# A gated cross attention kernel: scores moved behind the last attention segment, bias added in DRAM, inner sums moved ahead of three additions

## The chip, the cores and the metric

The kernel runs on one core of a Trainium2 chip. A core has five engines that run their own instruction streams side by side: TensorE (PE, matrix products; its weight loads are shown apart, as PEld), VectorE (DVE), ScalarE (ACT), GpSimd (POOL) and SyncE (SP, which here issues DMAs). The metric is the device time of one execution in microseconds, lower is better.

## What is computed

With `x` of 8 x 1024 x 1024 and a memory `ctx` of 8 x 64 x 512, all in float32:

```python
memory_proj = einsum('bme,de->bmd', memory, W_mem)
scores = einsum('bnd,bmd->bnm', x, memory_proj) / sqrt(D)
attn = softmax(scores, axis=-1)
memory_context = einsum('bnm,bmd->bnd', attn, memory_proj)
gate_input = concatenate([x, memory_context], axis=-1)
gate = sigmoid(einsum('bnf,df->bnd', gate_input, W_gate) + b_gate)
fused = x + gate * memory_context
out = fused * rsqrt(mean(square(fused), axis=-1) + 1e-6) * norm_w
```

D is 1024, M (the rows of memory of a batch) is 64. The large product is `x` by the first half of `W_gate`, 8192 x 1024 x 1024. The second half of `W_gate` is folded into the memory first: `mg = memory_proj @ W2` for each batch, so that `attn @ mg` gives what the concatenated half contributes, with the bias added to the rows of `mg` (the rows of `attn` sum to 1).

## The kernel before

**Quads and products.** The rows of `x` go through in 16 *quads* of 512 rows, two to a batch (`QPB` is 2, `NQ` is 16). The large product of a quad is done by a scheme of Strassen's kind, on two levels. On the outer level, seven products replace eight. They run in the order 1, 6, 7, 5, 4, 2, 3 (`ORDER`), and each is computed by `outer_product` (line 746). On the inner level, each outer product is again seven products of 128 x 256 blocks, named A, B, C, D, A (added onto the first), E and F; each of these takes one *slot* of TensorE. A quad has 49 slots.

**The left sides.** The four parts of the transposed `x` of a quad are `a11`, `a12`, `a21`, `a22` (`A[q, r, h]`), made by VectorE's transposes (`transpose_x`, line 335) out of the loaded rows `xq`. The sums that the outer products need, `S1` to `S4`, are VectorE's work over 1024 elements (`outer_s`, line 350): S1 = a21 + a22, S2 = S1 - a11, S3 = a11 - a21 (written in place of a21), S4 = a12 - S2. Outer product 7 takes S3 and outer product 3 takes S4. The sums for the inner products, four to an outer product in a tile `l2`, are GpSimd's work (`inner_s`, line 379), in two parts of two sums; B needs the first part, C and F the second.

**What follows a product.** ScalarE copies the first A to `u` (line 803), VectorE adds B, C and D onto it (`u2`, `u3`, `u4`). `pre` (line 785) adds `u3` and `u4` onto the output tiles on GpSimd, three additions for most outer products and six for product 5. `fin` (line 791) adds the PSUM results onto them on VectorE. Five PSUM banks are passed round from product to product, so that a late `fin` holds up a later product. The output tiles (`gate`) come from a pool of 7.

**The attention.** `scores(q)` (line 391) multiplies the memory with the `a` tiles: 16 pairs of matmuls, each pair using two column halves of the array (the weights have 64 columns), and ScalarE copies the result `psT`. It is emitted at slot 7 of the quad, between outer products 1 and 6. `transpose_scores`, `softmax_a`, `softmax_b`, `transpose_attn` and `attn_difference` follow at slots 9 to 21. In the last four outer products (5, 4, 2, 3), between the second A and E, stands a segment `pc` (line 820): eight pairs of matmuls, each on two row halves of the array (contraction over 64), which multiply the attention with the memory (`pc`) and with `mg` (onto A, F, E and D). Then ScalarE applies the sigmoid, and VectorE multiplies with `pc` (`gated`).

**The order of the work.** Nothing is left to a scheduler: `pin` keeps program order on every engine. `plan` (line 598) writes work into two lists. `at(slot, fn)` puts it into a slot, counted from `t0 = 49 * q`; it is emitted just before that slot's product. `mid((q, o), fn)` puts it into the middle of outer product `o` of quad `q`, behind the `pc` segment and before E. Later, `outer_product` itself plans `gated`, the residual (line 652, a GpSimd DMA that adds `x` onto the output tile while it loads), `square` (ScalarE) and `norm` (VectorE), which stores the tile. An engine runs its stream in order, so an instruction that waits holds up everything behind it on the same engine.

**The memory's side.** `mgd` is a DRAM tile of 2 x 512 x 1024: `mgd[0]` holds `memory_proj` and `mgd[1]` holds `mg` for all batches. `load_mg` (line 462) brings the 64 rows of each for a batch into one SBUF tile `mgs[b]`, at the beginning of the batch. `add_bias` (line 467) then adds the bias onto the upper 64 partitions by an accumulating GpSimd DMA, at slot 8 of the first quad of each batch, 8 times in all.

Of the kernel before, what the change touches and what calls it, by code (L numbers as in the profile page):

```python
# [10 lines left out]
ALU = mybir.AluOpType  # L11
# [4 lines left out]
P = 128  # L16
# [4 lines left out]
def tile_gated_cross_attention_rmsnorm(  # L21
# [42 lines left out]
    nc = tc.nc  # L64
    B, N, D = x.shape
    M, E = mem.shape[1:]
    QT = 4 * P
    QPB = N // QT
# [20 lines left out]
    pin = tc.keep_in_program_order  # L89
# [10 lines left out]
    def t4k(pool, shape, tag, name):  # L100
        return pool.tile(shape, F32, tag=tag, name=name)
# [33 lines left out]
    for k in range(KD):  # L135
        t = t4k(*((gpool, [P, D], "gate") if k < 7 else (apool, [P, D], "s4")), f"w2_{k}")
# [47 lines left out]
    mgd = dram.tile([2, BM, D], F32, name="mgd")  # L184
# [146 lines left out]
    sTs, attns, attnTs, scs, mps, mgs = {}, {}, {}, {}, {}, {}  # L331
# [132 lines left out]
        for g in range(2):  # L464
            load(mgs[b][g * M : (g + 1) * M, :], mgd[g, b * M : (b + 1) * M, :])

    def add_bias(b):
        pin(nc.gpsimd.dma_start(mgs[b][M:P, :], b_gate.partition_broadcast(M), accum_op=ALU.add))

# [116 lines left out]
    def at(slot, fn, *args):  # L588
        due.setdefault(slot, []).append(lambda: fn(*args))

    def mid(key, fn, *args):
        beside.setdefault(key, []).append(lambda: fn(*args))
# [5 lines left out]
    def plan(q):  # L598
        t0 = SLOTS * q
        nxt = q + 1 < NQ  # L600
        order = [o for o, _ in ORDER]
        for i, o in enumerate(order):
            for part, t in ((0, 1), (1, 5)):
                if i + 1 < len(order):
                    at(t0 + 7 * i + t, inner_s, q, order[i + 1], part)
                elif nxt:
                    at(t0 + 7 * i + t, inner_s, q + 1, order[0], part)
        at(t0 + 7, scores, q)
        at(t0 + 7, outer_s, q, 3)
        at(t0 + 7, outer_s, q, 4)  # L610
        at(t0 + 9, transpose_scores, q)
        at(t0 + 10, softmax_a, q)
        at(t0 + 13, softmax_b, q)
        at(t0 + 18, transpose_attn, q)
        at(t0 + 21, attn_difference, q)
        if not nxt:
            at(t0 + 5, load_last)
            return
        at(t0 + 2, load_xq, q + 1)
        for t in (2, 3):  # L620
            mid((q, 5), transpose_x, q + 1, t, 0)
            mid((q, 2), transpose_x, q + 1, t, 1)
        for i, t, half in ((36, 0, 0), (38, 1, 0), (43, 0, 1), (45, 1, 1)):
            at(t0 + i, transpose_x, q + 1, t, half)
        mid((q, 3), outer_s, q + 1, 1)
        mid((q, 3), outer_s, q + 1, 2)
        if (q + 1) % QPB == 0:
            at(t0 + 10, load_mp, (q + 1) // QPB)
            at(t0 + 49, load_mg, (q + 1) // QPB)
        if q % QPB == 0:  # L630
            at(t0 + 8, add_bias, q // QPB)

    for o in (2, 3):
        w1_place(o)
# [106 lines left out]
    def sqrt_table():  # L741

        t = t4k(small, [P, 1], "warm", "warm")
        pin(nc.scalar.activation(t, eps_sb, AF.Sqrt))  # L744

    def outer_product(q, o, ext):
# [113 lines left out]
        if o in (4, 3) and q + 1 == NQ:  # L860
            c, d = 2 * ext[0], 2 * ext[0] + 1
            if o == 3:
                sqrt_table()
            when = (4, 5, 7, 9, 11, 12) if o == 4 else (2, 4, 5, 6, 7, 8)
            at(slot + when[0], last_root, d)
            at(slot + when[1], last_root, c)
            for w_, (t, h_) in zip(when[2:], ((d, 0), (d, 1), (c, 0), (c, 1))):
                at(slot + w_, last_norm, t, h_)
        elif o in (4, 3):

            row = ext[0]
            c, d = 2 * row, 2 * row + 1
            for t in (d, c):
                at(slot + 5, residual, q, t)
            if row == 0:
                when = (17, 18, 23, 29, None, None)
            else:
                when = (17, 18, 23, 25, 26, 28)
            at(slot + when[0], square, q, c)
            at(slot + when[1], square, q, d)  # L880
            for w_, (t, h_) in zip(when[2:], ((c, 0), (c, 1), (d, 0), (d, 1))):
                if w_ is None:
                    mid((q + 1, 4), norm, q, t, h_)
                else:
                    at(slot + w_, norm, q, t, h_)
# [3 lines left out]
    for q in range(NQ):  # L889
        plan(q)  # L890
        for o, ext in ORDER:
            outer_product(q, o, ext)
# [29 lines left out]
```

## Time and profile before

| | |
|---|---|
| median of 3 runs | 974.6 us (974.18 to 974.84) |
| the profiled execution | 974.45 us, its span 972.7 us |
| TensorE busy | 961.5 us, 99% of the span |
| VectorE, GpSimd, ScalarE busy | 825.1, 763.4, 327.0 us |
| granted TensorE clock | 0.996 |
| scores (`psT`) | 512 matmul records, 16 x 32 |
| bias DMAs | 8, 256 KB each, 7.3 us to landing, 0.83 us of GpSimd each |
| residual DMAs | 60, 512 KB each, 8.2 us to landing (median) |
| from one quad's scores to the next | 55.05 us for most (87.12 to 142.31 is 55.19, 857.91 to 913.22 is 55.31) |

The *span* runs from the first to the last instruction of one execution that the hardware profiler recorded. A float32 matmul shows as two records, so a slot of two matmuls shows as four. In the chain of waits the profile follows what ended last back to the beginning; work that isn't in it was hidden. In a list of waits, a row says which engine and tile waited, for whom, how long in all, how often and how long at most. In a timeline a row has start, duration, engine, line, operation, tiles, shape and count; the ends of matmuls are modelled, so their starts are what counts. Rows with "issue" show idle time in which nothing recorded was waited for.

### The profile page before, as it was taken

The numbers are of one execution on the slowest core, as the hardware profiler recorded it, in microseconds if no ns is written. First come the engines' busy times: TensorE is split into PE (matmuls) and PEld (weight loads), VectorE is DVE, ScalarE is ACT, GpSimd is POOL, SyncE is SP. The second block draws the span as 40 slices with busy tenths as digits, with TensorE's granted clock in tenths as the row PEclk, the third lists the DMA queues.
The fourth block names the chain that finished last, engine by engine and source line by source line (L and its number), as shares of the span: only waits on it lengthen the run. The fifth ranks groups of instructions, "written<-read, shape, count | busy, mean of one in ns | idle before, by whom it ended". The sixth has DMA issues, their size and how long they took to land.

```text
span 972.7 us, 14393 instructions
## 1 busy us (share of the span) xinstructions
PE 961.5 (99%) x4986; PEld 772.9 (79%) x4986; DVE 825.1 (85%) x1483; ACT 327.0 (34%) x603; POOL 763.4 (78%) x895
## 2 busy tenths in 40 slices
PE   9999999999999999999999999999999999999995
PEld 8546878888888888888887888888887888888884
DVE  5988888979797988979797988979797988979787
ACT  2000224251423334151433334161333334152355
POOL 4998878878687878878787877878787887878792
PEclk9999999999999999999999999999999999999998
DMA  9857183573819373482818374481918465391612
GB/s 377 267 145 167 18 139 92 121 170 79 177 59 177 116 130 98 111 183 68 181 65 163 109 142 109 99 194 57 192 65 152 121 130 119 87 206 47 181 77 86
DMA packets 71255, 128.32 MB, mean 132 GB/s; under 512 B 12432, under 2 KB 49296, under 8 KB 70928
## 3 DMA queue, kind: packets, MB, share of 16 engines
q1 hardware_dynamic: 61760, 93.34, 35.4%
q0 software_dynamic: 9280, 33.56, 18.7%
q8 instruction: 39, 0.64, 0.3%
q10 hardware_dynamic: 144, 0.52, 0.2%
q14 instruction: 32, 0.26, 0.1%
HBM read 87.56 MB, written 39.85 MB: 131 GB/s over the span
## 4 chain that ended last, share of the span: by engine, by line
PE 99%; DVE 0%; ACT 0%; DVEq 0%; issue 0%
PE kA L92 20%; PE pc L92 12%; PE kE L92 11%; PE kD L92 10%; PE kF L92 10%; PE kC L92 10%; PE kB L92 10%; PE psT L92 6%; PE pg L92 5%; PE pm L92 3%; PE pz L92 0%; PE sc L412 0%; PE pa L438 0%; PE pt L194 0%; DVE gate L737 0%; ACT L744 0%
## 5 line engine op out<-in xcount | busy, mean ns | idle before, releaser
L95 POOL TENSOR_TENSOR gate<-gate,u 128x256 f32<-128x256 f32 x336 | 271.9, 841 | 112.0 <-DVE u L95 106.4
L650 ACT ACTIVATE gate<-gate 128x512 f32<-128x512 f32 x128 | 78.9, 629 | 399.3 <-DVE gate L95 399.2
L95 POOL TENSOR_TENSOR l<-a 128x256 f32<-128x256 f32 x128 | 132.1, 1032 | 55.6 <-DVE a L95 55.6
L344 DVE STREAM_TRANSPOSE a<-xq 128x512 f32<-128x512 f32 x128 | 137.7, 1097 | 3.1 <-DMA mgd<-mpq 3.1
L92 PE MATMUL pc<-mg,attnT 64*128 64x256 f32 x512 | 127.4, 389 | 0.0
L679 DVE SCALAR_TENSOR_TENSOR gate<-gate,ss,nw_sb 128x512 f32<-128x512 f32 x120 | 125.6, 1056 | 1.1
L92 PE MATMUL kB<-it,l 128*128 128x256 f32 x448 | 115.1, 379 | 0.0
L92 PE MATMUL kD<-it,l 128*128 128x256 f32 x448 | 115.0, 379 | 0.0
L92 PEld LDWEIGHTS pc<-mg,attnT 64*128 64x128 f32 x512 | 90.6, 186 | 29.8 <-issue 21.2
L92 PE MATMUL kA<-w,a 128*128 128x256 f32 x384 | 98.6, 379 | 0.0
L92 PEld LDWEIGHTS kB<-it,l 128*128 128x128 f32 x448 | 85.0, 190 | 11.8 <-DVE gate L95 0.3
L92 PEld LDWEIGHTS kD<-it,l 128*128 128x128 f32 x448 | 85.1, 190 | 11.6
L95 DVE TENSOR_TENSOR gate<-gate,pc 128x512 f32<-128x512 f32 x128 | 87.0, 679 | 5.9 <-ACT gate L650 5.8
L92 PEld LDWEIGHTS kA<-w,a 128*128 128x128 f32 x384 | 71.7, 190 | 9.5 <-DVE mg_c L95 0.2
L95 POOL TENSOR_TENSOR l<-s 128x256 f32<-128x256 f32 x96 | 75.3, 785 | 4.0 <-PE kF L92 3.8
L803 ACT COPY u<-kA 128x256 f32<-128x256 f32 x112 | 40.5, 362 | 103.5 <-PE kA L92 102.4
L92 PE MATMUL kE<-it,a 128*128 128x256 f32 x256 | 69.0, 392 | 0.0
L92 PE MATMUL kA<-t,s 128*128 128x256 f32 x256 | 67.4, 386 | 0.0
L95 DVE TENSOR_TENSOR u<-u,kB 128x256 f32<-128x256 f32 x112 | 45.4, 405 | 25.8 <-PE kB L92 23.8
L92 PE MATMUL kC<-w,l 128*128 128x256 f32 x256 | 65.7, 379 | 0.0
L92 PE MATMUL kF<-w,l 128*128 128x256 f32 x256 | 65.7, 379 | 0.0
L664 ACT ACTIVATE junk<-gate 128x1024 f32<-128x1024 f32 x60 | 63.6, 1059 | 1.5 <-DMA gate<-in_x 0.5
(140 smaller groups left out, 2036.0 us busy)
## 6 DMA issues: line engine op xcount, KB each, us to landing
xq<-in_x SPq DMA_DIRECT2D x64, 512.0 KB, 9.7
gate<-in_x POOLq DMA_DIRECT2D x60, 512.0 KB, 8.2
out<-gate SPq DMA_DIRECT2D x60, 512.0 KB, 2.6
w<-in_w_gate_t SPq DMA_DIRECT2D x8, 512.0 KB, 10.9
w<-in_w_gate_t SPq DMA_DIRECT2D x2, 2048.0 KB, 16.9
mg<-mgd SPq DMA_DIRECT2D x16, 256.0 KB, 3.8
mpd<-mpT SPq DMA_DIRECT2D x4, 512.0 KB, 7.0
mgd<-mpq SPq DMA_DIRECT2D x16, 128.0 KB, 4.2
```

Source lines behind the costliest of these rows:

```text
L92: pin(nc.tensor.matmul(o, lhsT, rhs, start=start, stop=stop, skip_group_check=True))
L95: pin(eng.tensor_tensor(o, a, b, op))
L344: nc.vector.transpose(A[key][:, :, r * P : (r + 1) * P], chunks(xq[q][:, 4 * t : 4 * t + 4, :], KD)[:, half * KH : (half + 1) * KH],)
L650: pin(nc.scalar.activation(g, g, AF.Sigmoid))
L664: nc.scalar.activation(junk, O[q, t], AF.Square, accum_out=ss[:, t % 2 : t % 2 + 1])
L679: nc.vector.scalar_tensor_tensor(g[:, cols], g[:, cols], rstd[:, t % 2 : t % 2 + 1], nw_sb[:, cols], ALU.mult, ALU.mult,)
L803: pin(nc.scalar.copy(p1, kb["A"]))
```

## The change

It has five parts.

1. `scores(q + 1)` is emitted in the middle of outer product 3 of quad `q`, behind its `pc` segment, for all quads but the first, whose scores stay at slot 7.
2. The third and fourth outer sums, which were at slot 7 with the scores, go to slots 6 and 20 for all quads but the first.
3. Of the four transposes for the next quad with fixed slots, the last two go from slots 43 and 45 to 42 and 43.
4. The bias is added in SBUF for the first batch only. For the others one accumulating GpSimd DMA over 448 rows adds it in DRAM, onto `mgd[1, 64:]`, at slot 20 of the first quad.
5. The second part of the inner sums of the outer product behind 7 (which is 5) goes from slot 19 to slot 16, and with that ahead of the three additions of product 7. The last two norms of the tiles of outer product 4 go three and four slots back (`when`, 26 to 29 and 28 to 32).

```diff
-    def add_bias(b):
-        pin(nc.gpsimd.dma_start(mgs[b][M:P, :], b_gate.partition_broadcast(M), accum_op=ALU.add))
+    def add_bias(rows):
+        pin(
+            nc.gpsimd.dma_start(
+                rows, b_gate.partition_broadcast(rows.shape[0]), accum_op=ALU.add
+            )
+        )
...
-            for part, t in ((0, 1), (1, 5)):
+            for part, t in ((0, 1), (1, 2 if o == 7 else 5)):
...
-        at(t0 + 7, scores, q)
-        at(t0 + 7, outer_s, q, 3)
-        at(t0 + 7, outer_s, q, 4)
+        if q == 0:
+            at(t0 + 7, scores, q)
+        at(t0 + (6 if q else 7), outer_s, q, 3)
+        at(t0 + (20 if q else 7), outer_s, q, 4)
...
-        for i, t, half in ((36, 0, 0), (38, 1, 0), (43, 0, 1), (45, 1, 1)):
+        for i, t, half in ((36, 0, 0), (38, 1, 0), (42, 0, 1), (43, 1, 1)):
             at(t0 + i, transpose_x, q + 1, t, half)
+        mid((q, 3), scores, q + 1)
         mid((q, 3), outer_s, q + 1, 1)
         mid((q, 3), outer_s, q + 1, 2)
...
-        if q % QPB == 0:
-            at(t0 + 8, add_bias, q // QPB)
+        if q == 0:
+            at(t0 + 8, add_bias, mgs[0][M:P, :])
+            at(t0 + 20, add_bias, mgd[1, M:, :])
...
-                when = (17, 18, 23, 25, 26, 28)
+                when = (17, 18, 23, 25, 29, 32)
```

## The prediction

> **What bounds the kernel now.** I read the page first: busy times, then the chain that ended last.
>
> ```profile
> span 972.7 us, 14393 instructions
> ...
> PE 961.5 (99%) x4986; PEld 772.9 (79%) x4986; DVE 825.1 (85%) x1483; ACT 327.0 (34%) x603; POOL 763.4 (78%) x895
> ...
> PE 99%; DVE 0%; ACT 0%; DVEq 0%; issue 0%
> ```
>
> TensorE carries 99% of the chain. Only something that shortens TensorE's own sequence, or makes it wait, can count. Next, the waits, keeping TensorE's and those the change touches:
>
> ```profile
> PEld kE L92 <- issue: 21.2, 64, 0.3
> DVE a L95 <- PE psT L92: 23.1, 16, 1.5
> PEld kA L92 <- DVE a L95: 5.8, 15, 0.4
> PEld psT L92 <- issue: 5.3, 16, 0.3
> PEld kC L92 <- POOL l L95: 0.4, 1, 0.4
> ```
>
> Of TensorE's own, the `psT`, `kA` and `kE` rows recur in every quad at the same 0.3 to 0.4 us. They stand where the matmul's shape changes, so they are no data waits: the one called "DVE a" looks like the `kE` ones that wait for nothing. VectorE's 23.1 us behind `psT` is real, but VectorE is not in the chain. To price a shape change, the timeline of TensorE around a 64-row segment (`pc`) and around the 64-column scores (`psT`):
>
> ```profile
> 343.40 1.03 PE L92 MATMUL kA<-w,a 128*128 128x256 f32 x4
> 344.36 0.48 PE L92 MATMUL pc<-mg,attnT 64*128 64x256 f32 x1
> ...
> 344.68 0.38 PE L92 MATMUL pc<-mg,attnT 64*128 64x256 f32 x1
> ...
> 345.97 0.38 PE L92 MATMUL pc<-mg,attnT 64*128 64x256 f32 x1
> ...
> 346.29 1.13 PE L92 MATMUL kE<-it,a 128*128 128x256 f32 x4
> 347.25 1.03 PE L92 MATMUL kF<-w,l 128*128 128x256 f32 x4
> ```
>
> ```profile
> 361.47 1.03 PE L92 MATMUL kF<-w,l 128*128 128x256 f32 x4
> 362.42 3.67 PE L92 MATMUL psT<-a,mpb 128*64 128x256 f32 x32
> 366.03 1.13 PE L92 MATMUL kA<-t,s 128*128 128x256 f32 x4
> 366.99 1.03 PE L92 MATMUL kB<-it,l 128*128 128x256 f32 x4
> ```
>
> Starts are what to read. An undisturbed product of four records takes 0.863 us (347.25 to 348.12), 0.216 a record; two half-array records run side by side in 0.216.
> - `pc` segment: 343.40 to 347.25 is 3.85; two products (1.726) and 8 pairs (1.728) leave **0.40** for going in and out.
> - `psT` segment: 361.47 to 366.99 is 5.52; two products and 16 pairs (3.456) leave **0.34**.
> - Ways out: 345.97 to 346.29 is 0.32, so 0.10 over a pair; the next product starts after 0.96, another 0.10: 0.20. The way out of `psT` has the same 0.96 behind it. So the way into `pc` costs 0.40 - 0.20 = 0.20 and into `psT` 0.34 - 0.20 = 0.14. Both start 0.09 late; the rest is the first weights, unhidden (137 ns for 64 columns, 187 for 128, in the groups by shape).
>
> **What the skill says.** "TensorEngine Tiling (Array Packing)", Key Properties: "Mode switching requires drain", and it means a change of tiling mode. The trace agrees (0.14 to 0.20 a switch), but neither shows a switch from 64-row to 64-column tiles. "TensorE: Matmul & The Clock Gate", LDWEIGHTS pull-ahead in Step-by-step: weights load ahead while row groups don't conflict; between equal shapes the trace has weight loads 26 ns apart, at a switch 0.33 us. "GPSIMD Engine Reference", Specifications, lists its SBUF interfaces as shared with VectorE instructions that have two SBUF inputs; here the same GpSimd sum takes 0.72 to 1.05 us by what VectorE does. "DMA: Bandwidth & Descriptors", Queues, rings and completion order: each engine alternates between queues by packet; I use it for the accumulating loads below (their landing times rise from 5 to 15 us beside other loads, which fits).
>
> **The change, part by part.**
>
> *Scores moved (15 of 16 quads).* The same 32 records now follow the `pc` segment of the quad before, ahead of `kE`. Before, each quad paid 0.40 + 0.34. Now it pays the way into `pc` 0.20, one switch from row to column tiles, and the way out 0.20. That switch is not in the trace. Below: 0, if both tilings coexist; above: 0.34, as much as going out and in again; worse is conceivable only if it drains more than two switches do. I take 0.14, the way into `psT` (the drain of 0.09 and the same small weights). Saved: 0.74 - 0.54 = 0.20 a quad, 15 x 0.197 (unrounded) = **2.95 us**; ends 0 and 15 x 0.34 = 5.1. Scores need the second half of the transposes. VectorE runs them in slots 42 and 43 now: from `kF`'s sum at 348.39 in the same quad, transpose, `gated`, transpose end near 351.5, and the scores can start at 354.4: cover 2.9 us. ScalarE's copy of `psT` moves along, ahead of two sigmoids that wait for `kE` and `kF` anyway, 3.6 us later than before.
>
> *What that shifts.* Product 1 of the next quad runs 3.4 us later; from product 6 on all is 0.2 early again. So the cover that the scores gave at slot 7 is gone there and stands before product 1. GpSimd's residual DMA for tile 0 starts behind a VectorE product 2.6 us later (359.95 becomes 362.6). It landed 11 to 15 us after issue (7 in the last quad) and its square started 13.8 to 14.7 after; half of the quads have 0.0 to 1.1 us left. Its rival traffic (`xq`) starts about 1.1 us earlier, behind earlier transposes, and the bias DMA is gone from these quads, so the queues drain at about the same time. A square up to 1.1 us late is absorbed by ScalarE's 0.58 us wait before `u` and VectorE's own lag; TensorE needs the attention 2.3 us later.
>
> *Third and fourth outer sums, norms.* `outer_s 3` (1.22 us) no longer waits for `psT`; it ends at 366.65 instead of 365.65, for a GpSimd sum whose `kC` has 1.0 us of margin and gets its additions earlier too. `outer_s 4` (1.22) moves from behind `psT`'s wait, where it was free, to slot 20. The norm of slot 12 goes to slot 15, that of 14 to 18. All within VectorE's stretch from `u` of product 6 (368.13) to `u` of product 5 (380.66), which held 1.0 us of idle. After: it starts 0.4 earlier and holds 1.25 more work, so it ends near 380.8, 0.4 us later against TensorE. Behind it stand `u3` of product 5, GpSimd's six additions and the inner sum for `kC` of product 4. In before that sum ended 0.92 us ahead of its `kC` (387.62 against 388.55), bound by GpSimd's queue; 0.2 to 0.4 of it goes, 0.5 to 0.7 stays. Cost on the path 0.
>
> *Inner sums of product 5 ahead of three additions.* This is the tightest place before:
>
> ```profile
> 379.40 0.73 POOL L95 TENSOR_TENSOR l<-s 128x256 f32<-128x256 f32 x1
> ...
> 380.39 1.03 PE L92 MATMUL kC<-t,l 128*128 128x256 f32 x4
> ```
>
> 0.26 us of margin, -0.25 once (the `kC <- POOL` wait, at 875.96). The two sums (0.73 + 0.91) move into 1.54 us in which GpSimd waited for `u`, so they end some 3 us earlier and the additions hardly later. Gain: that one stall, **0.25 us**.
>
> *Bias.* Eight GpSimd DMAs of 64 rows (0.83 us each) become one of 64 and one of 448 rows into DRAM. Issue cost of 448: from 0.83 (64 rows) and 0.87 (128), an estimate of 1.1; 5.8 if it goes by row (0.83 x 448/64). In the first quad it stands before product 4's sums, where GpSimd idled 1.89 us (105.43 to 107.32), so 1.1 is free; 5.8 would cost TensorE 3.6 once, past the 0.3 us that product 4's `kC` has there. Transfer: 256 KB landed in 7.3 us, 512 in 8.2, so 1.8 MB in about 13 by that slope: landed before the first residual 17 us later, long before the next `mg` load 78 slots on. The gone DMAs save 6 x 0.83 us of GpSimd off the path.
>
> **The sum.** Profiled execution 974.45 us, span 972.7 (1.75 around it); 972.7 - 2.95 - 0.25 = 969.5 of span, 971.25 with what lies around. The median shown is 0.15 above the profiled execution: **971.4 us**, 0.33% less.
>
> **Rivals.** *The switch eats it:* going from row to column tiles costs 0.34 and only the stall of 0.25 is saved: 974.3, the same within 0.2% (about what a measurement of this kernel can tell from no change). For it: no such switch is in the trace. Against it: all four kinds seen cost 0.14 to 0.20. It turns from faster to same when the switch costs over 0.22. *Column tiles come free:* switch 0, 974.6 - 5.35 = 969.3. Against it: every change of shape has drained.
> *VectorE becomes late (slower):* place, `u3` of product 5 after `outer_s 4` and the moved norm; both lengthen beside GpSimd, the norm from 0.75 to 1.25. If the additional 1.25 us finds none of the 1.0 us idle and a norm takes 1.25 instead of 0.9, VectorE is 1.25 + 0.35 - 0.4 = 1.2 late, GpSimd's additions start so much later, and `kC` of product 4, with 0.7 us left, waits 0.5 in each of 15 quads: 7.5 on top, 978.9. It decides from a lateness of 0.7 (a stall) and 0.9 (15 x 0.2, the gain is gone). For it: VectorE is 85% busy and nearly without gaps there. Against it: the norms stay within the same stretch and its start is earlier.
> *The late residual:* squares wait over 3 us, the attention reaches `pc` late; 1 us in each of the 7 quads with `mg` loads, 978.4. Against it: the earlier `xq` and the missing bias DMA. *The change does nothing it says* is out: the instruction order has `psT` behind the last `pc` in 15 quads.
>
> **How the numbers follow.** Forecast 0.62 (switch 0.08 to 0.22, 970 to 972.6); free switch 0.07; switch eats it 0.17; VectorE late 0.08; residual or the long DMA 0.06, of which 0.02 still faster. Faster 0.62 + 0.07 + 0.02 = 0.71; same 0.17; slower 0.08 + 0.04 = 0.12. The range takes in the free switch's upper part and the equal case, and leaves out the slower ones: 969.5 to 974.6; the forecast's own is 970 to 972.6.
>
> **What would show it.** Quad period 54.85 instead of 55.05 us; the two `pc` and `psT` segments of a quad's end joined, the first `psT` 0.09 us late plus a first pair of 0.27; `PEld kA <- DVE a` from 5.8 to under 0.5; `DVE a <- PE psT` from 23.1 to about 1.5; no `kC <- POOL` in later quads; GpSimd's idle before product 7's additions gone. I am wrong if TensorE shows data waits of over 0.2 us in each quad, at `kC` of product 4 above all, or if the joint of the two tilings costs other than 0.14.

## The result and the profile after

The changed kernel takes **972.5 us** (median of 15 runs, 971.84 to 973.15), and the kernel before, run beside it, 974.5 us (15 runs, 973.95 to 974.97). The ratio is 0.998, with a 95% interval of 0.9973 to 0.9987: faster by 0.2%, or 2.0 us. The forecast was 971.4 us, so the gain is 1.2 us smaller than forecast. The profiled execution of the changed kernel took 972.48 us, its span is 970.7 us.

The page of the kernel after, its first lines and the chain that ended last:

```profile
span 970.7 us, 14400 instructions
...
PE 958.1 (99%) x4986; PEld 773.3 (80%) x4986; DVE 815.0 (84%) x1483; ACT 329.2 (34%) x603; POOL 763.5 (79%) x889
...
PE 97%; DVE 1%; DMA 1%; issue 0%; ACT 0%; DVEq 0%
```

TensorE still carries the chain. Its busy time fell by 3.4 us (961.5 to 958.1), the span by only 2.0: the rest stands as idle time. VectorE and a DMA at the kernel's start are in the chain now, with 1% each.

The list of waits of the kernel after (engine, tile, waited for what: us in all, times, longest us), keeping those of TensorE that changed and VectorE's wait for the scores:

```profile
PEld kE L92 <- issue: 22.0, 64, 0.4
PEld psT L92 <- issue: 5.3, 16, 0.3
DVE a L95 <- PE psT L92: 0.9, 1, 0.9
PEld kB L92 <- DVE gate L95: 0.8, 1, 0.8
PEld kC L92 <- POOL l L95: 0.5, 2, 0.3
PEld kA L92 <- DVE a L95: 0.4, 1, 0.4
PEld kD L92 <- DVE u L95: 0.4, 1, 0.4
```

The fifteen ways out of the scores, which stood as `kA <- DVE a` with 5.8 us before, are down to one. `psT` is as before and `kE` nearly so (21.2 before), so what went is one change of array mode in each of 15 quads. Of data waits inside the quads TensorE had two before, one at `kB` (0.3) and one at `kC` (0.4). Now there are four: `kB` once, `kC` twice, `kD` once. These are the losses.

The start times of TensorE's `sc` (the transposed scores) give a clock for the quads. The time from one quad's `sc` to the next:

| stretch | before | after | difference |
|---|---|---|---|
| up to the first `sc` | 92.48 | 92.45 | -0.03 |
| first quad | 55.19 | 55.54 | +0.35 |
| 13 quads between | 13 x 55.05 | 11 x 54.85, 54.91, 55.03 | -2.36 |
| last but one | 55.30 | 54.85 | -0.45 |
| from the last `sc` to TensorE's last matmul | 43.73 | 44.22 | +0.49 |
| sum | | | -2.00 |

The new joint, in TensorE's timeline of the kernel after (start, duration, engine, line, operation, tiles, shapes, count):

```profile
353.65 0.38 PE L92 MATMUL pc<-mg,attnT 64*128 64x256 f32 x1
353.66 0.38 PE L92 MATMUL kD<-mg,attnT 64*128 64x256 f32 x1
353.87 0.38 PE L92 MATMUL pc<-mg,attnT 64*128 64x256 f32 x1
353.88 0.38 PE L92 MATMUL kD<-mg,attnT 64*128 64x256 f32 x1
354.18 3.67 PE L92 MATMUL psT<-a,mpb 128*64 128x256 f32 x32
357.79 1.13 PE L92 MATMUL kE<-it,s 128*128 128x256 f32 x4
358.75 1.03 PE L92 MATMUL kF<-w,l 128*128 128x256 f32 x4
```

A pair of row halves takes 0.216 (353.65 to 353.87). From the last pair to the first `psT` it is 0.31 (353.87 to 354.18), so 0.09 late. From 354.18 to 357.79 the 16 pairs and the way out's first part take 3.61: 3.456 for the pairs, 0.05 for a first pair that is longer, and 0.10 to `kE`. The switch costs 0.09 + 0.05 = **0.14 us**, the value taken in the forecast; the second half of the way out (`kE` to `kF` 0.96 instead of 0.863) is there as before.

### The profile page after: what moved, and what is told of

Read it like the earlier page. It is cut to its first block, busy times and chain, and to the rows that moved or that the text cites. A ratio compares the mean times of both kernels' runs of the same rounds, so it can differ in the third digit from the quotient of the medians.

```text
span 970.7 us, 14400 instructions
## 1 busy us (share of the span) xinstructions
PE 958.1 (99%) x4986; PEld 773.3 (80%) x4986; DVE 815.0 (84%) x1483; ACT 329.2 (34%) x603; POOL 763.5 (79%) x889
## 4 chain that ended last, share of the span: by engine, by line
PE 97%; DVE 1%; DMA 1%; issue 0%; ACT 0%; DVEq 0%
PE kA L92 20%; PE pc L92 12%; PE kE L92 11%; PE kD L92 10%; PE kF L92 10%; PE kC L92 10%; PE kB L92 10%; PE psT L92 6%; PE pg L92 5%; PE pm L92 3%; DMA memq<-in_mem 1%; PE pa L438 0%; PE sc L412 0%; DVE gate L744 0%; DVE it L95 0%
## 5 line engine op out<-in xcount | busy, mean ns | idle before, releaser
L95 POOL TENSOR_TENSOR gate<-gate,u 128x256 f32<-128x256 f32 x336 | 287.5, 886 | 107.2 <-DVE u L95 107.2
L95 POOL TENSOR_TENSOR l<-a 128x256 f32<-128x256 f32 x128 | 124.6, 974 | 21.6 <-PE kA L92 20.4
L92 PEld LDWEIGHTS pc<-mg,attnT 64*128 64x128 f32 x512 | 90.6, 186 | 29.9 <-issue 21.2
L686 DVE SCALAR_TENSOR_TENSOR gate<-gate,ss,nw_sb 128x512 f32<-128x512 f32 x120 | 109.0, 918 | 1.1
L95 POOL TENSOR_TENSOR l<-s 128x256 f32<-128x256 f32 x96 | 79.3, 826 | 33.1 <-PE kF L92 30.3
L95 DVE TENSOR_TENSOR gate<-gate,kE 128x256 f32<-128x256 f32 x112 | 45.5, 418 | 48.4 <-PE kE L92 42.3
L671 ACT ACTIVATE junk<-gate 128x1024 f32<-128x1024 f32 x60 | 63.5, 1059 | 11.2 <-DMA gate<-in_x 10.2
```

What stands on the lines that cost most here:

```text
L92: pin(nc.tensor.matmul(o, lhsT, rhs, start=start, stop=stop, skip_group_check=True))
L95: pin(eng.tensor_tensor(o, a, b, op))
L671: nc.scalar.activation(junk, O[q, t], AF.Square, accum_out=ss[:, t % 2 : t % 2 + 1])
L686: nc.vector.scalar_tensor_tensor(g[:, cols], g[:, cols], rstd[:, t % 2 : t % 2 + 1], nw_sb[:, cols], ALU.mult, ALU.mult,)
```

## The experiments

Two theories stood at the beginning.

- **Joint:** the gain is one change of array mode less per quad (0.197 us), because the scores touch the `pc` segment. The rival: the gain comes from the scores standing at another time, away from slot 7, wherever that is.
- **Lateness:** the missing 1.2 us are VectorE's and GpSimd's lateness, in the first quad by the long bias DMA, elsewhere by the fourth outer sum at slot 20. Against it stands the forecast's own step, by which neither costs TensorE anything.

Each run is compared with the kernel before (974.4 to 974.5 us in each group of runs). The diffs are against the kernel after, where not said otherwise.

### The scores without the joint

```diff
-        mid((q, 3), scores, q + 1)
+        at(t0 + 48, scores, q + 1)
```

Slot 48 is the product `kF`, so that one product, `kE`, stands between the two segments. All else is as in the changed kernel.

> The changed kernel with the scores one slot later, between E and F of outer product 3, so that full-array products stand on both sides of them. Theory of the joint: both ways in and out are paid again, 0.197 us in each of 15 quads, so 2.95 us slower than the changed kernel, about 975.4, a period of 55.05. Rival (the gain comes from where in time the scores stand, away from slot 7, and from what that frees on VectorE): as fast as the changed kernel, 972.5, since only 0.9 us of position differs.

Measured: 975.35 us, ratio 1.0009 (1.0001 to 1.0018). The quads take 55.05 us, as before the change. The list of waits of this kernel:

```profile
PEld pc L92 <- issue: 21.2, 64, 0.3
PEld kE L92 <- issue: 21.2, 64, 0.3
...
PEld kF L92 <- issue: 5.8, 15, 0.4
PEld psT L92 <- issue: 5.3, 16, 0.3
```

The 5.8 us of the way out of the scores are back, 15 times, now at `kF`. One product behind the place where the scores save 0.2 us a quad they save nothing, so the joint is what saves, and the rival falls. With all other parts of the change in it this kernel is 1.0 us slower than before (975.35 against 974.37): beside scores that save nothing, these parts save nothing either.

### The scores alone

Against the kernel before, only the scores are moved:

```diff
-        at(t0 + 7, scores, q)
+        if q == 0:
+            at(t0 + 7, scores, q)
...
+        mid((q, 3), scores, q + 1)
```

> The kernel before with nothing but the scores of the next quad moved behind the last `pc` segment. Theory of the joint (one change of array shape less in each of 15 quads): quad period 54.85 us instead of 55.05 where nothing waits, so 2.95 us less, about 971.5; it has neither the first quad's new stall of 0.55 us nor, with the outer sums still together at slot 7, the late `outer_s 4`. Rival (the gain needs the other moves, because VectorE or GpSimd fall behind without them): the period stays at 55.05 or above, with a data wait of TensorE in each quad, at `kC` of product 5 first, which had 0.26 us to spare.

Measured: **1015.27 us**, ratio 1.0418 (1.0404 to 1.0432). The rival came true, and far beyond its size. The first quad takes 54.85 us, so the joint saves its 0.2 us here too; then quads of 55.6 and of 60.1 to 60.5 alternate. Here is what happens in a long one, in the timelines of GpSimd, VectorE and TensorE of this kernel, ordered by start:

```profile
206.05 0.82 POOL L468 DMA_DIRECT2D mg<-in_b_gate  x1
206.62 2.36 POOL L95 TENSOR_TENSOR gate<-gate,u 128x256 f32<-128x256 f32 x3
206.88 4.68 DVE L681 SCALAR_TENSOR_TENSOR gate<-gate,ss,nw_sb 128x512 f32<-128x512 f32 x1
...
210.04 0.96 POOL L95 TENSOR_TENSOR l<-s 128x256 f32<-128x256 f32 x1
211.08 1.07 POOL L95 TENSOR_TENSOR l<-l,s 128x256 f32<-128x256 f32 x1
...
212.28 2.08 PE L92 MATMUL kB<-it,l 128*128 128x256 f32 x4 [3.56 <-DVE gate L95]
214.15 1.53 PE L92 MATMUL kC<-w,l 128*128 128x256 f32 x4
```

The bias DMA of the quad is issued at 206.05. GpSimd goes straight on with six sums in an unbroken row, to 211.00, and the next begins at 211.08. A norm of VectorE that starts in this row, at 206.88, takes 4.68 us, and ends 0.56 us after the row. It is 4.68 to 4.82 in all seven long quads; the usual time of a norm here is 1.10. Behind the norm stand the additions that empty the PSUM banks which product 7 takes over from product 6, and TensorE's `kB` of product 7 waits 3.56 us for them. Then the wait costs more: the four records of `kB` take 1.87 us (212.28 to 214.15), where 0.863 is usual, and part of `kC` runs as slowly: 0.427 a record instead of 0.216, 1.5 us in all here. The Trainium skill says of this ("TensorE: Matmul & The Clock Gate", What's actually happening) that TensorE's clock falls to half after an idle window of about 3.4 us; this trace fits that, with its records of twice the length after 3.56 us, and a mean clock over the span of 0.985 instead of 0.996. A later run (the changed kernel with the bias in SBUF) does not: there a wait of 1.99 us was enough, and the clock fell only after TensorE had worked for 1.4 us again (a granted clock of 0.51 from 869.8 to 873.0, behind a wait that ended at 868.17). So 3.4 us without work is not a threshold that these runs show.

### The scores and the bias

The next two separate the DMA from the rest. Both have the scores moved as above. The first also has the bias in DRAM as in the changed kernel, the second has the eight bias DMAs into SBUF, but at slot 14:

```diff
-            at(t0 + 8, add_bias, q // QPB)
+            at(t0 + 14, add_bias, q // QPB)
```

> The kernel before with the scores moved and the bias added in DRAM, nothing else. Theory (in the run with the scores alone, the bias DMA at slot 8 of every second quad made GpSimd start an unbroken row of sums just ahead of VectorE's norm, which then took 4.7 us instead of 1.1[...]): without those DMAs no norm over 2 us, all quads near the 55.6 us that the ones without a bias DMA had, about 983. Rival (the 4.7 us come from the order of VectorE's work, the DMA is not needed for them): every second quad stays near 60.3, 1015.

> The kernel before with the scores moved and the bias still added in SBUF by eight DMAs, but at slot 14 instead of 8. Theory (it is the place of the DMA just ahead of a two-input VectorE instruction that costs): if none starts right behind it, no norm over 2 us, quads near 55.6, about 983; if another two-input instruction starts there, that one is stretched instead. Rival (each such DMA costs VectorE some 4 us wherever it stands): every second quad near 60, 1015.

Measured: with the bias in DRAM 984.35 us, ratio 1.0103 (1.0089 to 1.0117); at slot 14, 989.37 us, ratio 1.0155 (1.0141 to 1.0169). The same stretch of the first of them, without the DMA ahead of the row:

```profile
206.56 2.54 POOL L95 TENSOR_TENSOR gate<-gate,u 128x256 f32<-128x256 f32 x3
207.37 1.14 DVE L686 SCALAR_TENSOR_TENSOR gate<-gate,ss,nw_sb 128x512 f32<-128x512 f32 x1
209.22 1.13 PE L92 MATMUL kB<-it,l 128*128 128x256 f32 x4
```

The same norm beside the same row takes 1.14 us. And in the second, at slot 14:

```profile
209.90 0.83 POOL L468 DMA_DIRECT2D mg<-in_b_gate  x1
210.27 1.50 DVE L95 TENSOR_TENSOR e<-e,den 128x256 f32<-128x256 f32 x1
210.47 1.01 POOL L95 TENSOR_TENSOR l<-s 128x256 f32<-128x256 f32 x1
211.56 0.81 POOL L95 TENSOR_TENSOR l<-l,s 128x256 f32<-128x256 f32 x1
...
211.92 0.41 PE L438 MATMUL pa<-ident,e 128*128 128x128 f32 x2 [0.81 <-DVE e L95]
```

The norm is no longer held, but what VectorE does beside the DMA now is: the softmax's product `e<-e,den` takes 1.50 to 1.52 us instead of 0.65, in 7 of 7, until the gap at 211.48, and the transposes of the attention wait 0.81 for it. Hence 56.5 us in these quads against 55.64 in the others. So the bias DMAs of the seven later batches cost 31 us more than one long DMA in the first quad when they stand at slot 8 (1015.27 against 984.35), and 5 us more at slot 14 (989.37 against 984.35). Both places move the same data; what differs is which VectorE instruction stands beside the issue and the row of sums behind it.

Without them, a quad still takes 55.64 us, 0.79 over the joint's 54.85. Every quad has three stalls: 0.28 at product 7's `kB`, 0.36 at product 5's `kC`, 0.12 at the transposes of the attention. What removes the first two comes next; the third is gone in each of the next three runs, so none of them shows what removes it. The scores don't wait for the transposes of `x` although these stand at slots 43 and 45 here (`psT <- issue` is 5.3 us as before), so moving those to 42 and 43 was not needed for that; it was not tried by itself.

### The outer sums back together, the inner sums back, the norms back

```diff
-        at(t0 + (6 if q else 7), outer_s, q, 3)
-        at(t0 + (20 if q else 7), outer_s, q, 4)
+        at(t0 + 7, outer_s, q, 3)
+        at(t0 + 7, outer_s, q, 4)
```

> The changed kernel with both outer sums back at slot 7, so it has the scores, the DRAM bias, the early inner sums, transposes and norms as changed. Theory (two sums of 1.2 us in a row at slot 7, with nothing to wait for there any more, make VectorE late for `kB` of product 7 by 0.3 us a quad): period near 55.15, about 977. Rival (only the bias and the inner sums are needed with the scores): 54.85, 972.5.

```diff
-            for part, t in ((0, 1), (1, 2 if o == 7 else 5)):
+            for part, t in ((0, 1), (1, 5)):
```

> The changed kernel with the inner sums of product 5 back at slot 19, behind the three additions. Theory (they were moved to where GpSimd idled; with the scores elsewhere VectorE's `u` comes 1.1 us earlier there): `kC` of product 5 has some 1 us of margin instead of 3.9, no stall, the additions end a little earlier: 972.5 or up to 0.5 less. Rival (this move is needed for the gain): a stall at `kC` of product 5 in each quad, a period above 54.85, 974 or more.

```diff
-                when = (17, 18, 23, 25, 29, 32)
+                when = (17, 18, 23, 25, 26, 28)
```

> The changed kernel with the last two norms back at slots 26 and 28. Theory (both places lie in the same stretch of VectorE's work, so only its order changes): `u` of product 7 some 1 us later, `kC` of product 4 with its margin of 0.25 about unchanged, 972.5 within 0.5. Rival (the moved norms are what took the margin): the margin back at 0.9 and the last quad 0.49 shorter, 971.8.

Measured, in this order: 976.63 us, ratio 1.0023 (1.0015 to 1.0032); 975.55 us, ratio 1.0011 (1.0002 to 1.0019); 972.29 us, ratio 0.9978 (0.9969 to 0.9988).

With both outer sums at slot 7 the quads take 55.17 us, with a stall of 0.29 at product 7's `kB` in every quad: 2.4 us of VectorE stand in front of its work for product 6. With the inner sums back at slot 19, the wait that the change took away once is there in every quad (list of waits):

```profile
PEld kC L92 <- POOL l L95: 5.5, 15, 0.7
```

In nearly all of these it is the sum for product 5's `kC`, which ends too late; the stall is 0.19 us, 0.09 of waiting and 0.10 by which the second record is late (its weight load starts 0.11 us behind the first record, where it starts with it elsewhere). The quads take 55.04, and the joint's gain is eaten up. My expectation of a margin of 1 us was wrong: in this kernel the three additions of product 7 run from 376.65 to 379.20, and the first of the two inner sums behind them takes 1.71 us instead of 0.73. The norms' later slots make no difference to the quads: 54.85 with them and without, and product 4's `kC` has 0.32 us of margin instead of 0.25.

So of the parts beside the joint, two are needed to keep its gain (the outer sums apart: 0.3 us a quad; the inner sums early: 0.2 us a quad), the bias has to leave slot 8, and the norms do nothing by themselves.

### The long bias DMA

Four runs: the bias in DRAM alone, against the kernel before; the changed kernel with the eight DMAs into SBUF at slot 8, with `add_bias` as in the kernel before; the changed kernel with both outer sums early; and this last one with the long DMA at slot 34 as well.

```diff
-        if q % QPB == 0:
-            at(t0 + 8, add_bias, q // QPB)
+        if q == 0:
+            at(t0 + 8, add_bias, mgs[0][M:P, :])
+            at(t0 + 20, add_bias, mgd[1, M:, :])
```

> The kernel before with nothing but the bias added in DRAM. Theory (the DMAs it drops are off the path, the long one stretches VectorE in the first quad): the first quad 0.3 to 0.55 us longer, all other quads unchanged, about 975.0. Rival (fewer DMAs help the residual loads and with them TensorE): some quads shorter than 55.05 us, under 974.3.

> The changed kernel with the bias again added in SBUF, eight times. Theory: the first quad 0.55 us shorter, the rest as in the changed kernel as long as the accumulating loads leave the residuals in time: about 972.0. Rival (without the DRAM addition the later residual loads land too late): ScalarE's waits for `gate<-in_x`, 10.2 us in 7 waits in the changed kernel, grow, and TensorE waits at the `pc` segment of product 5 in up to 7 quads, 973 or more.

```diff
-        at(t0 + (6 if q else 7), outer_s, q, 3)
-        at(t0 + (20 if q else 7), outer_s, q, 4)
+        at(t0 + (4 if q else 7), outer_s, q, 3)
+        at(t0 + (6 if q else 7), outer_s, q, 4)
```

> The changed kernel with the third and fourth outer sums at slots 4 and 6 instead of 6 and 20, where VectorE waited for TensorE before `kE` of product 1 and `kB` of product 6. Theory (the fourth sum at slot 20 made VectorE 0.4 us late and with it GpSimd's additions, which took the margin of `kC` of product 4 and shifted the last quad's work): margin of `kC` of product 4 back from 0.25 to 0.6 us or more, the stalls of 0.06 and 0.18 gone and most of the last quad's 0.49, so 0.5 to 0.7 us less, about 971.9. Rival (the margin went for another reason, the norms moved or the earlier inner sums): margin stays at 0.25, time 972.5.

```diff
-            at(t0 + 20, add_bias, mgd[1, M:, :])
+            at(t0 + 34, add_bias, mgd[1, M:, :])
```

> The same with the DRAM bias addition at slot 34 of the first quad instead of 20. Theory (its 0.99 us on GpSimd stretched VectorE's attention difference from 0.84 to 1.39 us and that delayed `kB` of product 4): the stall before that `kB` falls from 0.69 to 0.14 us, so another 0.55 us less, about 971.3. Rival (the stall has another cause, such as the earlier inner sums): it stays at 0.69, 971.9. Its 15 us of transfer now lie beside the residual loads; if they come too late, ScalarE's squares wait in the first quads.

Measured: bias alone 975.24 us, ratio 1.0008 (0.9999 to 1.0016), with a first quad of 56.04 (+0.85, where 0.3 to 0.55 was expected) and the others nearly as before; what is held beside the issue there is not the attention difference but a sum of VectorE's, `it<-w`, 1.93 us instead of 1.10. SBUF bias in the changed kernel 975.59 us, 3.6 above the expected 972.0, ratio 1.001 (1.0004 to 1.0017), over a wide range of 974.26 to 977.99: its first quad takes 54.85, but in its last quad with a bias DMA a norm is held again (3.91 us, behind the issue at 861.91), and that quad takes 58.79, by a wait of TensorE and the half clock behind it. The residual loads, which the rival named, are not the cause. So at slot 8 these DMAs cost 3 us even with the rest of the change. Outer sums at slots 4 and 6: 977.84 us, ratio 1.0035 (1.0022 to 1.0047); with the DMA at slot 34 also, 977.01 us, ratio 1.0026 (1.0016 to 1.0036).

In the first quad the DMA is settled. With it at slot 20 the first quad takes 55.54 in the changed kernel and 55.90 with the sums at 4 and 6; without it there, 54.85 and 55.22: 0.7 us. The place, in the timelines of the kernel after:

```profile
103.33 0.99 POOL L469 DMA_DIRECT2D mgd<-in_b_gate  x1
103.98 1.39 DVE L95 TENSOR_TENSOR attnT<-attnT 64x256 f32<-64x256 f32 x1
104.02 1.05 POOL L95 TENSOR_TENSOR l<-a 128x256 f32<-128x256 f32 x1
105.15 0.80 POOL L95 TENSOR_TENSOR l<-l,a 128x256 f32<-128x256 f32 x1
...
112.87 0.92 PE L92 MATMUL kB<-it,l 128*128 128x256 f32 x3 [0.42 <-DVE gate L95]
```

The issue takes 0.99 us (1.1 was the estimate), and GpSimd has the room. But VectorE's attention difference, which starts beside it, takes 1.39 us instead of 0.84 before, and VectorE is 0.55 later from there on, up to product 4's `kB`.

The early outer sums missed their expectation, and the reason is a third case of the same kind. GpSimd, VectorE and TensorE in a later quad of this kernel (sums at slots 4 and 6):

```profile
419.77 0.88 POOL L661 DMA_DIRECT2D gate<-in_x  x1 [0.71 <-DVE gate L95]
420.35 1.05 POOL L95 TENSOR_TENSOR l<-s 128x256 f32<-128x256 f32 x1
420.45 2.72 DVE L95 TENSOR_TENSOR a<-a,a 128x1024 f32<-128x1024 f32 x1
421.04 1.04 POOL L95 TENSOR_TENSOR l<-s,l 128x256 f32<-128x256 f32 x1
...
423.65 1.10 PE L92 MATMUL kB<-it,l 128*128 128x256 f32 x4
```

The third outer sum falls beside a residual DMA's issue and the sums behind it, and takes 2.72 us instead of 1.22; product 6's `kB` is late by 0.36 us in each quad (period 55.21). In the changed kernel it starts at slot 6, after this row, and takes 1.22. The other half of the expectation holds: with the fourth sum gone from slot 20, the margin of product 4's `kC` is 0.80 us instead of 0.25, and the last stretch takes 43.86 us instead of 44.22, close to the 43.73 of before.

### A version that is better than both

The DMA goes to slot 34, where VectorE has nothing to be held, and the last norm of the tiles of product 4 goes to slot 37, out of the tight stretch of VectorE ahead of product 5:

```diff
-            at(t0 + 20, add_bias, mgd[1, M:, :])
+            at(t0 + 34, add_bias, mgd[1, M:, :])
...
-                when = (17, 18, 23, 25, 29, 32)
+                when = (17, 18, 23, 25, 29, 51)
```

> The changed kernel with the last norm of outer product 4's tiles moved on to slot 37 of the next quad, out of VectorE's tight stretch and to where GpSimd idles 1.8 us, and with the DRAM bias at slot 34 of the first quad. Theory (VectorE late by 0.4 us took the margin of `kC` of product 4 and the last quad's 0.49 us; the long DMA the first quad's 0.68): margin back over 0.6, period 54.85 in all quads, the first 54.86, the tail 43.8: 971.2. Rival (the margin is GpSimd's and not VectorE's, as the run with the old norms suggests): margin stays at 0.25, only the first quad gains, 971.8; or the norm collides at its new place, period above 54.85.

Measured: **971.58 us** (971.30 to 971.95), ratio 0.9971 (0.996 to 0.9983). Its page begins:

```profile
span 969.8 us, 14386 instructions
```

All 15 quads take 54.85 us. The attention difference takes 0.54, product 4's `kC` has 0.43 to 0.82 of margin instead of 0.05 to 0.40, and the stalls of the first quad (0.69 us) and of the quads 6 and 8 (0.06 and 0.18) are gone: 0.93 together, where the medians differ by 0.92. The last stretch, 44.26 us, isn't better. In the changed kernel its 0.49 us are lost at one place: in the `pc` segment of product 4, `kD` waits for VectorE's `u` (the row `kD <- DVE u` of the list above). In this version 0.13 is left there and 0.11 and 0.29 stand at products 2 and 3. The loss at product 4 shrinks to about 0.1 us when the fourth outer sum leaves slot 20 (sums at slots 4 and 6) and also when the inner sums go back to slot 19. What makes products 2 and 3 late in this version was not tried by itself.

## Why the prediction was right, and where not

The direction, the size of the main term and the range (969.5 to 974.6) were right. By the prediction's steps:

- *The switch from row to column tiles:* taken at 0.14, measured 0.14, so 0.20 saved in each of 15 quads. The Trainium skill's statement ("TensorEngine Tiling (Array Packing)", Key Properties) that a change of tiling mode drains TensorE agrees with this switch as well: it isn't free. Both rivals on its price fall: it is neither free nor does it eat the gain. The period is the forecast 54.85.
- *Scores' cover at the new place:* right. No `psT` waits for the transposes; `psT <- issue` has the same 5.3 us.
- *The residual for tile 0 is late:* it is. It is issued at 363.29 instead of 359.95 and lands after up to 12.6 us; ScalarE's squares wait for it 7 times, 10.2 us in all and up to 2.2 each, instead of once. TensorE doesn't wait for it, as forecast.
- *The outer sums and norms at no cost:* **this step failed in its size.** I let the 1.25 us of new work take up VectorE's 1.0 us of idle and come out 0.4 late against TensorE, with 0.5 to 0.7 of margin left for product 4's `kC`. `u` of product 5, where that stretch of VectorE ends, begins 13.89 us behind the quad's `sc`, and 12.80 before the change: it is 1.09 late. The margin is 0.25 in most quads and below nothing in two of them (0.24 us), and the same lateness falls on the last quad (0.49). The sum had a fault of its own, too: a start 0.4 earlier, with 1.0 of idle used up and 1.25 of new work, ends at 380.5 and not at 380.8, and against TensorE the start is no earlier (0.27 us behind `sc` in both kernels). The idle time was not free to be used, as the timelines of the kernel after show:

```profile
375.92 0.74 DVE L686 SCALAR_TENSOR_TENSOR gate<-gate,ss,nw_sb 128x512 f32<-128x512 f32 x1
375.98 1.27 POOL L95 TENSOR_TENSOR l<-s,l 128x256 f32<-128x256 f32 x1
377.21 2.09 POOL L95 TENSOR_TENSOR gate<-gate,u 128x256 f32<-128x256 f32 x3
377.96 0.42 DVE L95 TENSOR_TENSOR gate<-gate,kD 128x256 f32<-128x256 f32 x1 [0.88 <-POOL gate L95]
378.99 1.40 DVE L95 TENSOR_TENSOR s<-a,s 128x1024 f32<-128x1024 f32 x1
381.28 0.42 DVE L95 TENSOR_TENSOR u<-u,kB 128x256 f32<-128x256 f32 x1
382.97 4.17 POOL L95 TENSOR_TENSOR gate<-gate,u 128x256 f32<-128x256 f32 x6 [1.13 <-DVE u L95]
```

  VectorE's additions of product 7 follow GpSimd's additions onto the same tiles. These begin at 377.21, 9.82 us behind `sc` (9.48 before), because the inner sums now stand ahead of them, and the second of these takes 1.27 us beside the moved norm. So VectorE's wait there grows from 0.23 to 0.88 us, and the outer sum behind it takes 1.40 instead of 1.22. I had costed the edits one by one, each at nothing; they meet in this wait. Three runs that each take one edit out of this stretch give most of the margin back; putting both norms back, which leaves them in the stretch, doesn't:

| run | `u` of product 5 behind `sc` | margin of product 4's `kC` |
|---|---|---|
| after | 13.89 us | 0.25 us |
| inner sums back at slot 19 | 12.88 | 0.82 |
| last norm moved out of the stretch (slot 37) | 13.37 | 0.77 |
| fourth outer sum out of slot 20 (slots 4 and 6) | 13.34 | 0.80 |
| both norms back, inside the stretch | 13.81 | 0.32 |

  That nothing worse came of it was luck. The prediction has the gain gone when VectorE is 0.9 late. It is 1.09 late, but only 0.67 reaches the margin: the norm behind `u` takes 0.75 us instead of 1.03, and before the change GpSimd was still busy with other sums for some 0.2 us when VectorE's `u` for the six additions was ready. Neither was in the forecast.
- *The inner sums early:* the forecast was a gain of one stall, 0.25, which came. Its worth was misjudged: without it the changed kernel stalls 0.19 us in nearly every quad. It is not a small gain but a condition for the large one.
- *The bias:* issue, landing (15.6 us, forecast 13) and GpSimd's room were right; the loss came by another way, VectorE held beside the issue, 0.55 us once. The prediction asked only what the DMA does to GpSimd.

The terms add up: 3.2 forecast, less 0.55 in the first quad, 0.24 in two quads and 0.49 at the end is 1.92, against 2.00 in the spans.

The rival *VectorE becomes late* had the right place and the right chain, and nearly the right lateness (1.2). It fell short of a stall by some 0.25 us in most quads: that near was the change to losing its gain.

## What to carry to other kernels

Where a kernel changes between array modes, put the segments with unusual modes side by side: what counted here is the number of changes, and a change from one half mode to the other cost no more here than one from the full array. Before moving work into an engine's idle time, look for what that idle time waits for: idle behind another engine's work moves with that work. And when a DMA is issued from GpSimd, look at which VectorE instructions with two inputs in SBUF stand beside the issue and the row of GpSimd work behind it; with the scores alone moved, six slots took back 26 of the 31 us that the bias DMAs cost.

## What the runs showed of the hardware

A VectorE instruction with two SBUF inputs that starts beside a GpSimd DMA issue with an unbroken row of GpSimd sums right behind it, or inside that row, is held until about the first gap in the row:

| kernel | VectorE instruction | beside such a row | else |
|---|---|---|---|
| scores alone | norm | 4.68 to 4.82 us, 7 of 7 | 1.14 (bias in DRAM) |
| outer sums at 4 and 6 | outer sum 3 | 2.72 to 2.73 us, all 15 | 1.22 (after) |
| bias at slot 14 | `e<-e,den` | 1.50 to 1.52 us, 7 of 7 | 0.65 (bias in DRAM) |
| bias alone | `it<-w` | 1.93 us, once | 1.10 (before) |
| after | attention difference | 1.39 us, once | 0.54 (DMA at slot 34) |
| before, first quad | `e<-e,den` | 1.73 us, once | 0.59 (bias at slot 14) |

The last row shows that the issue needn't be close. In the timelines of GpSimd and VectorE of the kernel before:

```profile
93.73 0.98 POOL L468 DMA_DIRECT2D mg<-in_b_gate  x1
97.42 1.73 DVE L95 TENSOR_TENSOR e<-e,den 128x256 f32<-128x256 f32 x1
97.88 0.98 POOL L95 TENSOR_TENSOR l<-s 128x256 f32<-128x256 f32 x1
98.94 0.80 POOL L95 TENSOR_TENSOR l<-l,s 128x256 f32<-128x256 f32 x1
```

`e<-e,den` begins 3.7 us behind the issue, but the row behind that issue has its first gap at 98.86, and the instruction ends 0.29 us later.

These rows have a mark in the traces. Within them GpSimd's records overlap, mostly by 0.29 to 0.37 us; in all 14 traces no two records of GpSimd overlap by over 0.1 us in a row that no DMA issue begins. 73 VectorE sums and norms with two SBUF inputs began beside such an issue or inside the row behind it. 72 of them ended behind the row's last sum: 0.29 us (256 elements), 0.56 (512) or 1.09 (1024). The exception is the attention difference with both outer sums at slot 7, which began 0.16 us ahead of the row's first sum and took 0.58; others that began up to 0.32 ahead of it were held.

`gate<-gate,pc`, which has one input in PSUM, stands beside the residual DMAs 30 times in the kernel before and takes 0.68 us in each. The Trainium skill ("SBUF — State Buffer", SBUF: two separate sides) says that GpSimd and a VectorE instruction with two SBUF inputs lock a shared pair of ports, each for a whole instruction, while the other waits. That only these instructions are held agrees with the traces. That the lock ends with one instruction doesn't: the norm waited through six sums. Beside a row without a DMA ahead it waited through none. What it is about a DMA issue that makes the next sums run into one another, and whether other work in the DMA's place would do the same, was not tried.
